# Attention branch sums finished in 32-row blocks on VectorE instead of by token through TensorE transposes

## Chip, core and metric

The kernel runs on one core of a Trainium2 chip. The metric is the device time of one execution in microseconds (us). A difference of less than about 0.3% cannot be told from none. The engines are TensorE (PE: matmuls and transposes, result in PSUM), VectorE (DVE), ScalarE (ACT), GpSimd (POOL, works on SBUF only here) and SyncE (SP, issues the DMAs).

## What is computed

The input x has 8 rows of 512 tokens of 256 numbers; everything is f32. It is normalised, and attention and a feed-forward part are added to it. Attention has 16 heads of 16 numbers and three branches: over 32 compressed keys (each made from 16 tokens), over the 4 best groups of 16 tokens, and over a causal window of 32 tokens back. Three gates per token weigh the branches.

```python
s_b = einsum('bhtd,bhnd->bhtn', q, k_c) / scale
logits_c = where(c_ok, s_b, NEG)                  # a group counts once it lies wholly in the past
out_c = einsum('bhtn,bhnd->bhtd', softmax(logits_c), v_c) * any(c_ok)
_, top_idx = top_k(logits_c, 4)                   # 4 groups of 16 tokens per query and head
out_s = ...                                       # softmax attention over the chosen tokens
wmask = (abs(pos[:, None] - pos[None, :]) <= 32) & (pos[:, None] >= pos[None, :])
out_l = einsum('bhts,bhsd->bhtd', softmax(where(wmask, q @ k / scale, NEG)), v)
gates = softmax(q.mean(axis=1) @ Wg + bg)         # three per token
out = gates[..., 0:1] * out_c + gates[..., 1:2] * out_s + gates[..., 2:3] * out_l
x = x + out @ Wo + ffn(xn)
```

The feed-forward part is a gated MLP of width 1024 and a product-key mixture over 1024 small experts (4 heads, 8 chosen of 64 x 64 pairs). The change does not touch it.

## The kernel before, in words

The work is cut into 8 rows and 32 blocks of 128 tokens (`tiles`: number `n`, position `i` = 0 to 3 in the row); the MLP goes by halves of a row. Each step is a Python generator (a stage), and `each` makes one chain per stage over its rows, blocks or halves. A planner, the `Conductor` (class before `tile_kernel`), holds a model of every engine's time: at each `yield` a stage says which engine and which buffers or events it needs next, `price` gives each instruction a length, and `run` issues the step that can begin first, the lower rank first among near ties. `PLAN` holds one number per item of each stage that shifts its rank. So prices and ranks fix, before the run, the order of the instructions in each engine's queue; on the chip each queue is worked strictly in that order. PSUM is handed out as two pairs of banks and four single banks (`pairs`, `banks`), SBUF buffers by `stock(name, count, shape)`.

The steps that matter here, for one block:

- `queries`: q, then the compressed logits: two matmuls of all 32 keys of 8 heads each, and a mask product; ACT copies them to `lg`.
- `select`: the maximum per head, the differences `ec` on POOL, the choice of the four groups.
- `compressed`: ACT takes exp of `ec`, PE turns it in four transposes (`ecT`), and four matmuls with `ecT` as the stationary operand multiply by `vc17`. The result lies by token (128 tokens in partitions, 17 numbers per head, the seventeenth the sum of the weights). DVE inverts the sums and scales by them and the gate: `atc`.
- `weights`: for the window (unit `None`) and for each key block: 16 matmuls of 32 rows by 128 columns (four heads side by side), exp on ACT into `wT`. To the window unit a band mask is added by four full 128x128 matmuls of an identity with `bandT`.
- `products`: `wT` times `v17` into two accumulator banks `acc[0]`, `acc[1]`. These have heads and numbers in partitions (32 per head group `g`: 16 numbers, then the sum of weights) and tokens in columns, for the two branches.
- `finish(0)` and `finish(1)`, through `by_token`: ACT copies an accumulator to `acs`, PE turns it by four transposes, DVE inverts the sums (`rzn`) and scales each branch by its gate (`at`), POOL adds the two branches and `atc`, PE turns the sum back by one transpose, ACT copies it to `attnT`.
- `project`: the experts' product and two matmuls with `attnT` into one bank, then DVE adds to `yo` and SP writes it out.

Per row, `prepare_values` makes `v17`, the copies of the 32 last tokens `vl17`, and `vc17`; `gates` makes `gt` (tokens in partitions; 3 gates by 4 blocks); `release_row` frees them. The line that the profile shows for nearly everything is that of the planner's helper (L202), so instructions are told apart by the names of their tiles.

Of the kernel before, what the change touches and what calls it, by code (L numbers as in the profile page):

```python
# [12 lines left out]
ALU = mybir.AluOpType  # L13
# [3 lines left out]
P = 128  # L17
# [25 lines left out]
    ("ident", P), ("any", 1), ("slot", 8), ("fold", 2 * P), ("head4", H), ("last", 2),  # L43
]
_BF_COLS = [
    ("identb", P), ("win", P + WIN), ("caus", P), ("causT", P), ("bandT", P), ("prevT", WIN),
# [17 lines left out]
def shape_constants():  # L64
# [21 lines left out]
    put("head4", p // NB == np.arange(H)[None] % 4)  # L86
# [6 lines left out]
    putb("bandT", np.where((q - p >= 0) & (q - p <= WIN), 0.0, OUT))  # L93
# [14 lines left out]
def bc(ap, axis, n):  # L108
# [8 lines left out]
    "-10",  # L117
    "-12",
    "-5 -5 2 -1 -3 -11 0 -1",
    "-30 5 0 -14 0 -5 12 -4",  # L120
    "0 7 6 -4 0 0 10 4",
    "-7 5 4 0 9 25 -10 6",
    "-1 3 -1 23 3 14 4 -30 -30 -2 -7 -11 -2 -20 4 3 -9 -6 30 1 3 -1 3 4 2 14 -7 2 6 -8 10 23",
    "-3 0 2 -4 8 0 0 -4 -2 0 -4 -1 -7 -4 1 0 3 2 0 -7 0 2 0 1 -21 -2 0 -3 23 -9 7 -10",
    "-1 0 24 30 12 4 10 0 29 4 -1 -30 5 3 1 0 20 26 6 30 0 9 1 13 18 -1 13 16 -10 16 28 21",
    "4 0 -5 0 0 3 3 -27 0 -5 -6 -30 -15 -28 2 -16 8 6 -13 9 -29 -25 0 -13 -17 12 3 -6 0 -14 28 "
    "2",
    "-1 7 7 0 11 -14 18 -30 0 -12 1 -12 -2 19 0 -7 8 0 0 0 7 0 6 -24 -24 -28 13 -19 10 -23 -21 "
    "7",
    "-19 -18 12 -8 0 -17 -3 -20 -19 3 1 0 -4 -14 -1 -12 -1 -26 9 2 7 5 -1 -2 3 -14 -9 -12 0 0 "  # L130
    "8 -11",
    "0 -4 -25 -23 4 -7 -17 -30 -30 -2 -1 -29 -13 -30 -2 -11 -24 0 -4 -27 -28 -30 9 -3 -9 -2 "
    "-27 0 0 -9 2 16",
    "0 -7 -21 -2 -1 -5 -7 -6 0 -30 0 -25 -3 -3 10 -3 7 0 17 15 6 12 0 0 0 2 22 5 29 -28 30 0",
    "-6 0 0 16 5 10 -8 5 17 -14 1 8 -26 -9 0 0 4 0 2 4 -10 -7 1 -3 14 -27 26 -3 15 2 -10 13",
    "-3 1 0 0 3 0 -3 -4 1 2 2 -30 0 -10 3 1 3 -5 0 -4 10 2 0 7 11 0 6 0 0 -2 14 28",
    "-14 9 -8 -1 -10 -3 1 27 -13 0 3 1 -7 1 -4 6 -12 -24 -2 1 3 -18 -6 7 21 1 -2 9 -13 0 4 15",
    "-2 -29 0 -7 3 -1 -30 0 0 -18 -3 0 11 0 11 -10 -12 0 -7 30 -27 -24 0 -3 -13 -1 16 8 1 -10 "
    "24 23",
    "-1 0 -10 0 0 -30 -7 18 -3 2 11 1 -11 11 -20 7 -7 4 0 7 8 -3 12 -5 0 4 -25 8 -25 0 -14 12",  # L140
    "20 1 0 -3 7 6 18 7 -18 4 -8 1 -14 -6 1 -8",
    "0 7 0 -7 0 -3 7 1 0 4 0 0 -2 -3 8 15",
    "-16 19 19 6 -10 6 -8 15 1 0 -5 1 7 6 12 21 -20 15 26 3 -4 -7 -1 -8 -9 -5 6 9 -9 -15 -25 0",
    "-28 10 -28 13 -3 0 4 -11 0 12 19 -21 -5 -14 28 -26 -2 0 26 17 13 -29 25 -23 17 0 0 26 -2 "
    "7 12 0",
# [60 lines left out]
class Conductor:  # L206
# [26 lines left out]
    def price(self, eng, op, args, kw):  # L233
# [3 lines left out]
        if eng == "PE":  # L237
            self.tiling = (P, P)
            if op == "transpose":
                cost = 0.109  # L240
            else:
                n = int(np.prod(args[2].shape[1:]))
                cost = n * 0.433e-3 if args[2].dtype == BF16 else max(n * 1.69e-3, 0.223)
                if self.share > 1:
                    k, m = args[1].shape[0], int(np.prod(args[1].shape[1:]))
                    self.tiling = tuple(32 if a <= 32 else 64 if a <= 64 else P for a in (k, m))
                    each = 1.05 if m > 32 else 0.97 if n > 64 else 1.25
                    cost = max(n * 0.423e-3 * each, 0.017)
        elif eng == "SP":
            cost = 0.36  # L250
        else:
# [4 lines left out]
            if eng == "POOL" and any(a.dtype == BF16 for a in aps):  # L256
                cost += 0.24e-3 * n
            if op in ("match_replace", "max_index", "tensor_tensor_reduce", "reciprocal"):
                cost += 0.08
# [69 lines left out]
def tile_kernel(ctx, tc, x, wq, wk, wqT, wv, wo, bdk, bdv, wga, bga, wgu, bg, bu, wd, bd,  # L329
# [64 lines left out]
    ident, identb = const("ident"), bconst("identb")  # L394
    cmask = bconst("cmask").rearrange("p (i n) -> p i n", n=NB)
# [37 lines left out]
    vc17s = stock("vc17_", 2, [P, H * D1])  # L433
    for st_, fill in ((v17s, 1.0), (vl17s, 0.0), (vc17s, 0.0)):
        for it in st_.items:
            pool.memset(it[0], fill)
# [5 lines left out]
    for it in vc17s.items:  # L442
        pool.tensor_copy(by_head(it[0])[:, :, D], const("head4"))
# [23 lines left out]
    gts = stock("gt", 3, [P, 3, NT])  # L467
# [8 lines left out]
    ecTs, acss = stock("ecT", 1, [P, 4, P]), stock("acs", 2, [P, 4, P])  # L476
    rzs = stock("rzn", 3, [P, 16])
    atcs, at2s = stock("atc", 2, [P, 16, D]), stock("at2", 2, [P, 2, 2, 4 * D])
# [178 lines left out]
    def gates(s, pg):  # L657

        s.gt = yield DVE, gts
        gt, gm = s.gt.ap, buf_gm  # L660
# [13 lines left out]
        vec.tensor_tensor(gt[:, 2, 0:1], gt[:, 2, 0:1], const("any"), ALU.mult)  # L674
        s.done("gates")
# [3 lines left out]
    def prepare_values(s):  # L679
# [53 lines left out]
        s.vc17 = yield None, vc17s  # L733
        vc17 = s.vc17.ap
        pt = yield PE, banks
        pvt = pt.ap[:, :2 * P].rearrange("p (c n) -> p c n", c=2)
        for f in range(2):
# [4 lines left out]
        vec.tensor_tensor(by_head(vc17)[:, :, :D], pvt.rearrange("p c (h d) -> p (c h) d", d=D),  # L742
                          bc(const("head4"), 2, D), ALU.mult)
# [7 lines left out]
    def release_row(s):  # L751
# [8 lines left out]
        for it in (s.vc17, s.v17, s.vl17):  # L760
            it.free()
        yield None, s.tiles[-1].ev("at0"), s.tiles[-1].ev("at1")
        s.gt.free()
# [3 lines left out]
    def queries(t):  # L767

        s, i = t.row, t.i
        yield None, s.ev("xn"), came["wq_s"]  # L770
# [13 lines left out]
        pt, t.lg = yield PE, banks, lgs  # L784
        for a in range(2):
            mm(pt.ap[:, a * 8 * NB:(a + 1) * 8 * NB], t.q.ap[:, a, :],
               s.kcbd.ap[:, a].rearrange("p h n -> p (h n)"), start=a == 0, stop=False,
               skip_group_check=True)
        pc = pt.ap.rearrange("p (h n) -> p h n", n=NB)
        first = i * (P // G)  # L790
        mm(pc[:, :, first:], identb, bc(cmask[:, i, first:], 1, H), start=False, stop=True,
           skip_group_check=True)
        yield ACT,
        act.copy(t.lg.ap[:, :, 4:], pc)
# [60 lines left out]
    def select(t):  # L855
# [13 lines left out]
        pool.tensor_tensor(t.ec.ap, lg[:, :, 4:], bc(mx, 2, NB), ALU.subtract)  # L869
# [68 lines left out]
    def by_token(acs, dst, gates):  # L938

        pt = yield PE, banks  # L940
        p4 = pt.ap.rearrange("p (a g d) -> p a g d", a=4, g=4)
        for a in range(4):
            pe.transpose(p4[:, a].rearrange("p g d -> p (g d)"), acs.ap[:, a, :], ident)
        acs.free()
        rzn = yield DVE, rzs
        po = p4.rearrange("p a g d -> p (a g) d")
        vec.reciprocal(rzn.ap, po[:, :, D])
        for b in range(2):
            c = slice(8 * b, 8 * b + 8)
            vec.scalar_tensor_tensor(dst[:, c], po[:, c, :D], gates[:, b:b + 1],  # L950
                                     bc(rzn.ap[:, c], 2, D), ALU.mult, ALU.mult)
        pt.free()
        rzn.free()

    def compressed(t):

        s, i = t.row, t.i
        yield ACT, t.ev("ec")
        act.activation(t.ec.ap, t.ec.ap, AF.Exp)
        pt, ecT = yield PE, banks, ecTs  # L960
        for g in range(4):
            pe.transpose(heads4(pt.ap)[:, g, :],
                         t.ec.ap[:, 4 * g:4 * g + 4, :].rearrange("p h n -> p (h n)"), ident)
# [4 lines left out]
        yield None, s.ev("vc"), s.ev("gates")  # L968

        pt = yield PE, banks  # L970
        w = 4 * D1
        for g in range(4):
            mm(pt.ap[:, g * w:g * w + w], ecT.ap[:, g, :], s.vc17.ap[:, g * w:g * w + w],
               start=g == 0, stop=g == 3, skip_group_check=True)
        ecT.free()
        t.done("pc")
        t.atc, t.attnT = yield None, atcs, attnTs
        rzn = yield DVE, rzs
        po = by_head(pt.ap[:, :H * D1])
        vec.reciprocal(rzn.ap, po[:, :, D])  # L980
        vec.scalar_tensor_tensor(t.atc.ap, po[:, :, :D], s.gt.ap[:, 2, i:i + 1], bc(rzn.ap, 2, D),
                                 ALU.mult, ALU.mult)
        pt.free()
        rzn.free()
        t.done("atc")

    def weights(t):
# [27 lines left out]
        for k in [None, *range(i // 2 * 2, i + 1), *range(i // 2 * 2)]:  # L1015
# [13 lines left out]
            mask = bconst("bandT") if k is None else bconst("causT")[:, :FEW] if i == 0 else None  # L1029
            if mask is not None:  # L1030
                for j in range(4):
                    mm(heads4(es[j // 2].ap[:, j % 2])[:, :, :mask.shape[-1]], identb, bc(mask, 1, 4),
                       start=False, stop=True, skip_group_check=True)
# [12 lines left out]
    def products(t):  # L1046
# [9 lines left out]
        accs = [a.ap.rearrange("p (b j q) -> p b j q", b=2, j=2) for a in acc]  # L1056
        for u in range(2 * (i + 2)):
# [3 lines left out]
            for jj in range(2):  # L1061
                for g in range(4):
                    c = D1 * (4 * g + 2 * jp + jj)
                    mm(accs[jp][32 * g:32 * g + 32, br, jj, :], v17[:n, kt, c:c + 32],
                       wT.ap[:n, jj, g, :], start=u < 2 and jj == 0, stop=False,
                       skip_group_check=True, tile_position=(0, 32 * g))
            wT.free()
            if u == 1 and i:
                for jp in range(2):
                    rows_ = slice(64 * jp, 64 * jp + 64)  # L1070
                    for jj in range(2):
                        for g in range(4):
                            c = D1 * (2 * g + jj)
                            mm(accs[jp][32 * g:32 * g + 32, 1, jj, :WIN], vl17[rows_, i - 1, c:c + 32],
# [6 lines left out]
    def finish(jp):  # L1081
        def body(t):
            s, i = t.row, t.i
            yield None, t.ev("pv"), t.ev("atc")
            acs, at2h = yield ACT, acss, at2s
            act.copy(acs.ap, heads4(t.acc[jp].ap))
            t.acc[jp].free()
            at2 = at2h.ap
# [329 lines left out]
```

## Time and profile before

| what | value |
|---|---|
| median of three timed executions | 1501.49 us (1499.8 to 1504.47) |
| the profiled execution's own time | 1506.37 us |
| its span, first to last instruction | 1504.3 us |
| mean granted TensorE clock | 0.989 |
| ACT, POOL busy | 649.0 us (43%), 962.5 us (64%) |
| DMA queue of the kernel's own transfers | 18.4% of 16 engines |

Busy time is the union of an engine's instructions, each from its start to its modelled end; consecutive instructions overlap by the pipeline's tail, so the mean length of one is more than what it costs in the queue. The chain that ended last is followed back from the last instruction, at each step to what released it. The group lines read: line, engine, operation, tile written <- tiles read, shape written <- shape read, count, then busy us, mean ns of one, then the idle time of the engine just before them and what ended most of it.

### The profile page before, as it was taken

How to read it: one execution, taken by the hardware profiler on the slowest of the kernel's cores; microseconds unless marked ns; L12 is line 12 of the kernel's file. 1: busy time of each engine (PE TensorE's matmuls, PEld its weight loads, DVE VectorE, ACT ScalarE, POOL GpSimd, SP SyncE). 2: the span in 40 equal slices, each digit the busy share in tenths (PEclk: the TensorE clock that was granted, in tenths of full speed). 3: DMA queues.
4: the chain of work that ended last, by engine and by line, in shares of the span. 5: the costliest groups of instructions: out<-in, count | busy, mean ns of one | idle time of the engine just before them, and what ended most of it. 6: DMA issues, size and time to landing. Idle time of an engine off the chain costs nothing.

```text
span 1504.3 us, 44379 instructions
## 1 busy us (share of the span) xinstructions
PE 1440.8 (96%) x17312; PEld 1126.9 (75%) x17312; DVE 1300.7 (86%) x5207; ACT 649.0 (43%) x1292; POOL 962.5 (64%) x948
## 2 busy tenths in 40 slices
PE   5899998999999999999999999999999999999999
PEld 4677777777777777777877778777877777877777
DVE  3989889979989988899889896989798978999992
ACT  3534451544354445452544425444434435344253
POOL 3546756755567566874675756777636775577676
PEclk9899999999999999999999999999999999999999
DMA  8111111212112112121122212022120112111120
GB/s 287 44 45 50 36 53 32 80 46 60 47 31 79 45 43 58 51 62 51 30 61 62 60 47 62 25 67 59 48 66 26 55 48 60 52 27 52 37 59 19
DMA packets 100018, 83.52 MB, mean 56 GB/s; under 512 B 23265, under 2 KB 80609, under 8 KB 99681
## 3 DMA queue, kind: packets, MB, share of 16 engines
q1 hardware_dynamic: 99808, 80.69, 18.4%
q8 instruction: 136, 2.23, 0.6%
q14 instruction: 74, 0.60, 0.1%
HBM read 49.67 MB, written 4.19 MB: 36 GB/s over the span
## 4 chain that ended last, share of the span: by engine, by line
PE 66%; DVE 24%; ACT 3%; issue 2%; POOL 2%; DMA 2%; SPq 0%; DVEq 0%; ACTq 0%; POOLq 0%
PE psum L202 66%; DVE bm L202 3%; DVE pick L202 2%; DVE big L202 1%; POOL big L202 1%; DVE sums L202 1%; DVE chosen L202 1%; DVE ml L202 1%; DVE at_x L202 1%; DVE aT L202 1%; ACT wT L202 1%; DVE hT L202 1%; DVE xg L202 1%; DVE mr L202 1%; DVE at L202 1%
## 5 line engine op out<-in xcount | busy, mean ns | idle before, releaser
L202 POOL TENSOR_TENSOR big<-chosen,ed 128x1024 f32<-128x1024 bf16 x128 | 275.1, 2149 | 250.1 <-DVE chosen L202 164.6
L202 ACT ACTIVATE wT<-psum 128x1024 f32<-128x1024 f32 (+1 forms) x224 | 218.4, 1024 | 149.6 <-PE psum L202 140.5
L202 PE MATMUL psum<-xnT,wb 128*128 128x256 f32 x1024 | 250.4, 388 | 9.2 <-DVE hT L202 6.9
L202 POOL TENSOR_TENSOR big<-big,ed 128x1024 f32<-128x1024 f32 x128 | 248.6, 1942 | 9.9
L202 PEld LDWEIGHTS psum<-xnT,wb 128*128 128x128 f32 x1024 | 187.4, 191 | 45.4 <-DVE hT L202 9.2
L202 DVE TENSOR_REDUCE bm<-psum 128x32 f32<-128x512 f32 (+2 forms) x224 | 199.5, 912 | 18.6 <-PE psum L202 18.2
L202 POOL TENSOR_TENSOR big<-big 128x512 f32<-128x512 f32 x128 | 141.0, 1102 | 9.6
L202 PE MATMUL psum<-wT,v 128*32 128x128 f32 (+1 forms) x3584 | 127.6, 278 | 7.4 <-ACT wT L202 5.3
L202 ACT ACTIVATE xg<-psum,bg_s 128x256 f32<-128x256 f32 x128 | 60.9, 476 | 162.0 <-PE psum L202 160.4
L202 PEld LDWEIGHTS psum<-xnT,deT_s 128*128 128x128 f32 x1024 | 122.1, 193 | 10.5 <-issue 4.9
L202 PE MATMUL psum<-xnT,deT_s 128*128 128x128 f32 x1024 | 127.0, 277 | 0.0
L202 PE MATMUL psum<-wd_s,hT 128*128 128x256 f32 x512 | 124.7, 387 | 1.2 <-DVE hT L202 0.8
L202 PE MATMUL psum<-ue_s,aT 128*128 128x256 f32 x512 | 121.8, 384 | 0.2 <-DVE aT L202 0.2
L202 PEld LDWEIGHTS psum<-wT,v 128*32 128x32 f32 (+1 forms) x3584 | 90.5, 110 | 40.3 <-ACT wT L202 16.5
L202 DVE SCALAR_TENSOR_TENSOR aT<-aT,psum 128x512 f32<-128x512 f32 x128 | 86.6, 680 | 27.3 <-ACT aT L202 23.5
L202 PEld LDWEIGHTS psum<-ue_s,aT 128*128 128x128 f32 x512 | 94.0, 190 | 21.3 <-issue 5.4
L202 PEld LDWEIGHTS psum<-wd_s,hT 128*128 128x128 f32 x512 | 94.0, 192 | 20.6 <-issue 4.2
L202 PE MATMUL psum<-k,q 32*128 32x384 f32 (+3 forms) x1024 | 98.0, 474 | 5.8 <-DMA k<-kT 5.7
L202 DVE TENSOR_TENSOR chosen<-rc 128x1024 bf16<-128x1024 bf16 x128 | 99.4, 776 | 0.0
L202 POOL TENSOR_TENSOR gw<-big 128x256 f32<-128x256 f32 x128 | 90.6, 707 | 10.0
L202 PE MATMUL psum<-qx,k 32*128 32x128 f32 (+1 forms) x2560 | 94.3, 282 | 1.8 <-ACT wT L202 1.3
L202 PEld LDWEIGHTS psum<-qx,k 32*128 32x128 f32 (+1 forms) x2560 | 78.4, 182 | 21.9 <-issue 14.6
(158 smaller groups left out, 2911.3 us busy)
## 6 DMA issues: line engine op xcount, KB each, us to landing
wb<-in_wgu SPq DMA_DIRECT2D x128, 256.0 KB, 2.7
qx<-qT SPq DMA_DIRECT2D x96, 64.0 KB, 1.9
qx<-xT SPq DMA_DIRECT2D x96, 64.0 KB, 1.9
yo<-in_x SPq DMA_DIRECT2D x32, 128.0 KB, 2.1
q<-qT SPq DMA_DIRECT2D x64, 64.0 KB, 2.0
k<-kT SPq DMA_DIRECT2D x16, 256.0 KB, 2.5
out<-yo SPq DMA_DIRECT2D x32, 128.0 KB, 1.7
kw<-k SPq DMA_DIRECT2D x48, 80.0 KB, 2.5
```

Source lines behind the costliest of these rows:

```text
L202: return f(*a, **k)
```

## The change

`by_token` and its ten transposes per block are gone. The accumulators' columns are laid out in four blocks of 32 tokens, so that a DVE transpose of 32x32 blocks puts 32 tokens into the 32 partitions of each head group. The compressed product is made in the same layout: `vcq` is now the stationary operand and `ecT` streams. Three such turns fill `accT` (branch, token block, head in the group, 32 numbers). A new stage `join` inverts all 48 sums in one reciprocal, multiplies by the gates, has POOL scale all three branches and add them, and turns the sum back with a fourth DVE transpose straight into `attnT`. The gates are needed per head group and token block, so `gates` has SP copy them in 16 small transfers per row into `gx`. The rows of Wo are put in the new order on the host.

The band mask becomes sixteen 32x32 matmuls, each on its own tile of the array. `queries`, `select` and `compressed` work on the `nb` = 8(i+1) compressed keys that block `i` can see, where they had all 32. The planner has two new prices, and `PLAN` is replaced in all 23 stages and has a 24th for `join`.

```diff
-    ("identb", P), ("win", P + WIN), ("caus", P), ("causT", P), ("bandT", P), ("prevT", WIN),
+    ("identb", P), ("win", P + WIN), ("caus", P), ("causT", P), ("bandR", 4 * P), ("prevT", WIN),
...
+                if self.share > 4:
+                    cost = max(n * 0.433e-3 / 16, 0.017)
...
+            if eng == "POOL" and op == "memset":
+                cost = 0.08 + 0.85e-3 * n
...
-    vc17s = stock("vc17_", 2, [P, H * D1])
+    vcqs = stock("vcq", 2, [P, 4, P])
...
-    gts = stock("gt", 3, [P, 3, NT])
+    gts, gxs = stock("gt", 1, [P, NT, 3]), stock("gx", 3, [P, 4, NT, 3])
...
-    ecTs, acss = stock("ecT", 1, [P, 4, P]), stock("acs", 2, [P, 4, P])
-    rzs = stock("rzn", 3, [P, 16])
-    atcs, at2s = stock("atc", 2, [P, 16, D]), stock("at2", 2, [P, 2, 2, 4 * D])
+    ecTs, accTs = stock("ecT", 1, [P, 4, P]), stock("accT", 1, [P, 3, 4, 4, 32])
+    rz3 = buf("rz3", [P, 3, 4, 4])
+    ats = stock("at", 1, [P, 16, D])
...
+        s.gx = yield SP, gxs
+        for c in range(4):
+            for g in range(4):
+                sp.dma_start(out=s.gx.ap[32 * g:32 * g + 32, c], in_=gth.ap[32 * c:32 * c + 32])
...
         for a in range(2):
-            mm(pt.ap[:, a * 8 * NB:(a + 1) * 8 * NB], t.q.ap[:, a, :],
-               s.kcbd.ap[:, a].rearrange("p h n -> p (h n)"), start=a == 0, stop=False,
-               skip_group_check=True)
-        pc = pt.ap.rearrange("p (h n) -> p h n", n=NB)
+            mm(pc[:, 8 * a:8 * a + 8], t.q.ap[:, a, :], s.kcbd.ap[:, a, :, :nb], start=a == 0,
+               stop=False, skip_group_check=True)
         first = i * (P // G)
-        mm(pc[:, :, first:], identb, bc(cmask[:, i, first:], 1, H), start=False, stop=True,
+        mm(pc[:, :, first:], identb, bc(cmask[:, i, first:nb], 1, H), start=False, stop=True,
            skip_group_check=True)
...
-    def by_token(acs, dst, gates):
-
-        pt = yield PE, banks
-        p4 = pt.ap.rearrange("p (a g d) -> p a g d", a=4, g=4)
-        for a in range(4):
-            pe.transpose(p4[:, a].rearrange("p g d -> p (g d)"), acs.ap[:, a, :], ident)
...
-        w = 4 * D1
-        for g in range(4):
-            mm(pt.ap[:, g * w:g * w + w], ecT.ap[:, g, :], s.vc17.ap[:, g * w:g * w + w],
-               start=g == 0, stop=g == 3, skip_group_check=True)
+        pc = pt.ap.rearrange("p (b j q) -> p b j q", b=4, j=4)
+        for j in range(4):
+            mm(pc[:, :, j, :], s.vcq.ap[:, j, :], ecT.ap[:, j, :].rearrange("p (b q) -> p b q", b=4),
+               start=j == 0, stop=j == 3, skip_group_check=True)
         ecT.free()
         t.done("pc")
...
+        t.accT = yield DVE, accTs
+        vec.transpose(t.accT.ap[:, 2].rearrange("p b j m -> p (b j m)"), pt.ap)
         pt.free()
...
-            mask = bconst("bandT") if k is None else bconst("causT")[:, :FEW] if i == 0 else None
-            if mask is not None:
+            if k is None:
+                con.share = 16
+                for c in range(4):
+                    for j in range(4):
+                        r = slice(32 * j, 32 * j + 32)
+                        mm(heads4(es[j // 2].ap[32 * c:32 * c + 32, j % 2]), identb[r, r],
+                           bc(bandR[r, c], 1, 4), start=False, stop=True, skip_group_check=True,
+                           tile_position=(32 * j, 32 * c))
+                con.share = 1
...
-            yield None, t.ev("pv"), t.ev("atc")
-            acs, at2h = yield ACT, acss, at2s
-            act.copy(acs.ap, heads4(t.acc[jp].ap))
+            yield DVE, t.ev("pv"), t.ev("acc2")
+            vec.transpose(t.accT.ap[:, 0:2, :, 2 * jp:2 * jp + 2, :].rearrange("p r b j m -> p r b (j m)"),
+                          t.acc[jp].ap.rearrange("p (r b n) -> p r b n", r=2, b=4))
             t.acc[jp].free()
...
+    def join(t):
+
+        s, i = t.row, t.i
+        yield None, s.ev("gates")
+        yield DVE, t.ev("acc0"), t.ev("acc1")
+        acc = t.accT.ap.rearrange("p r b j m -> p r (b j) m")
+        vec.reciprocal(rz3.rearrange("p r b j -> p r (b j)"), acc[:, :, :, D])
+        vec.tensor_tensor(rz3, rz3, bc(s.gx.ap[:, :, i, :].rearrange("p b r -> p r b"), 3, 4), ALU.mult)
+        t.done("rz")
+        yield POOL,
+        part = t.accT.ap.rearrange("p r b j m -> p (r b j) m")[:, :, :D]
+        pool.tensor_tensor(part, part, bc(rz3.rearrange("p r b j -> p (r b j)"), 2, D), ALU.mult)
+        pool.tensor_tensor(acc[:, 0, :, :D], acc[:, 0, :, :D], acc[:, 1, :, :D], ALU.add)
+        ath = yield POOL, ats
+        at = ath.ap
+        pool.tensor_tensor(at, acc[:, 0, :, :D], acc[:, 2, :, :D], ALU.add)
+        t.accT.free()
+        t.attnT = yield DVE, attnTs
+        vec.transpose(t.attnT.ap.rearrange("p a (b q) -> p b a q", b=4),
+                      at.rearrange("p (b a j) d -> p b a (j d)", b=4, a=2))
+        ath.free()
+        t.done("attn")
...
-        yield PE, t.ev("attn0"), t.ev("attn1")
+        yield PE, t.ev("attn")
...
+    each(tiles, lambda t: t.n + 0.24, join)
```

## Prediction

> **What bounds the kernel now.** I read the page's busy table first, then the chain that ended last, then the timeline of one block's end, then the groups with shapes kept apart.
>
> ```profile
> PE 1440.8 (96%) x17312; PEld 1126.9 (75%) x17312; DVE 1300.7 (86%) x5207; ACT 649.0 (43%) x1292; POOL 962.5 (64%) x948
> ...
> PE 66%; DVE 24%; ACT 3%; issue 2%; POOL 2%; DMA 2%; SPq 0%; DVEq 0%; ACTq 0%; POOLq 0%
> ```
>
> TensorE (PE) has work for 96% of the span and owns 66% of the chain. VectorE (DVE) is second in both: 86% and 24%. So work taken from PE should show, and work given to DVE is dear. The table by stretches says how dear:
>
> ```profile
> 400.00:600.00 200.00, 193.99 (x2544) 151.10 (x2542) 180.61 (x732) 92.33 (x179) 126.80 (x123) 1.00 0.18 50
> 600.00:800.00 200.00, 196.98 (x2323) 153.33 (x2322) 178.59 (x749) 88.34 (x178) 133.56 (x133) 1.00 0.17 49
> ```
>
> (columns: length, then busy us of PE, its weight loads, DVE, ACT, POOL, then clock, DMA share, GB/s). In the body PE is at 97 to 98% and DVE at 89 to 90%. The clock is 1.00, so there is nothing to win from it. Over 40 to 1400 us the rows sum to PE 1317.6 and DVE 1211.1 of 1360: 97% and 89%.
>
> **The removed end of a block**, in the timeline (start, length, engine, what):
>
> ```profile
> 673.53 1.07 ACT L202 COPY acs<-psum 128x512 f32<-128x512 f32 x2
> 674.94 0.91 PEld L202 LDWEIGHTS psum<-cst,acs 128*128 128x128 f32 x8
> 675.05 1.04 PE L202 MATMUL psum<-cst,acs 128*128 128x128 f32 x8
> 675.69 0.26 DVE L202 RECIPROCAL rzn<-psum 128x16 f32<-128x16 f32 x1
> 675.98 0.61 DVE L202 SCALAR_TENSOR_TENSOR at<-psum,gt,rzn 128x128 f32<-128x128 f32 x2
> 676.67 0.45 POOL L202 TENSOR_TENSOR at<-at 128x128 f32<-128x128 f32 x1 [1.16 <-DVE at L202]
> ```
>
> A "mean ns of one" on PE (276 for this form) holds a pipeline tail that the next matmul overlaps; what one costs in the queue is the spacing: 1.04 us for eight, of which the last one's length is 0.273, so 0.767/7 = 0.110 us each.
>
> **PE, per block of 128 tokens (32 blocks).**
> - Ten transposes go (two times four of acs, two of at): 10 x 0.110 = 1.10 us.
> - The band mask is four 128x512 bf16 matmuls now: four in 1.04 us in the timeline, (1.04 - 0.39)/3 = 0.217 each, 0.87 in all. It becomes sixteen matmuls of 32 rows x 32 columns that stream 512 columns each. The trace has 32x32 tiles only with 32 columns: 32 of them in 0.45 us, or 11.3 us for 768, 15 ns each. Lower bound: issue, 16 x 0.015 = 0.24. Upper bound: the four column groups take turns, 4 x 0.217 = 0.87, no gain. I take issue of most of them plus one stream, about 0.40, nearer to the row of its own tile shape; gain 0.47, bounds 0 to 0.63.
> - Against this stands the Trainium skill, "TensorE: Matmul & The Clock Gate", section "Why this matters for your kernels": sixteen 32x32 tiles at 512 columns measured 660 ns as a set. By it the gain is 0.21 instead of 0.47, and the whole sum 8 us smaller; no row here shows the set.
> - Compressed logits: four passes of 256 columns per block at 0.217 (the kcbd group) become 64, 128, 192 or 256 columns by block position. A 128-column pass has a spacing of 0.11 (the deT_s group, 127.0 us for 1024, tails included) and I allow no less for 64. Gain 4 x (0.107 + 0.107 + 0.054 + 0)/4 = 0.27. Their mask falls from 512/384/256/128 to 128 columns: mean gain 0.08.
> - The vc product streams 128 columns instead of 68. Both sit at the 0.11 floor: 0. The products keep their columns, only in blocks of 32: 0.
> - Sum 1.10 + 0.47 + 0.27 + 0.08 = 1.92 us; x 32 = **61 us off PE** (bounds 46 to 66).
>
> **DVE.** These three groups go:
>
> ```profile
> L202 DVE SCALAR_TENSOR_TENSOR at<-psum,gt,rzn 128x128 f32<-128x128 f32 x128 | 39.0, 347 | 2.6
> L202 DVE RECIPROCAL rzn<-psum 128x16 f32<-128x16 f32 x96 | 24.0, 250 | 17.0 <-PE psum L202 16.6
> L202 DVE SCALAR_TENSOR_TENSOR atc<-psum,gt,rzn 128x256 f32<-128x256 f32 x32 | 15.5, 484 | 1.4
> ```
>
> 78.5 us. In their place, per block: three 32x32-block turns of 128x512 out of PSUM, one of 128x256 out of SBUF, one reciprocal and one product of 128x48. The trace has no turn. The rows that read the same 128x512 from PSUM are 680 (aT) and 683 ns (bm), the 128x256 SBUF reduction is 418. If the turn passes an element as these do, 3 x 0.68 + 0.42 = 2.46. From below I see no reason for less than the 593 ns in which ACT copies such a bank, 0.27 less per block, 9 us in all. From above the DVE row with the most time per element is the contended pick product, 873 ns for 256, 3.4 ns per element: 1792 elements x 2.4 ns more = 4.3 us per block. I take 2.46, nearest in source and shape. The Trainium skill, "Vector Engine (DVE) Microarchitecture Reference", section 3.8 on the reshape front end, says the turn sustains one element per cycle per lane; by its rate the middle value holds, and no run here shows it. The reciprocal lies between 0.25 (16 elements) and 0.46 (rising on as from 4 elements at 173 to 16 at 250): 0.33. The product lies between 265 (32 elements) and 374 (64): 0.32. Sum 3.11 x 32 = 99.5; net **+21 us on DVE**, 1322 in all (bounds +8 to +165).
>
> **ACT, POOL, SP.** ACT loses acs (35.5) and attnT (17.0) and parts of the ec and lg passes: about 58 us off an engine at 43%; worth nothing by itself, but wT exponentials start sooner behind it. POOL loses its two at groups (33.9 + 32.3) and about 10 us of ec (1104 ns at 512 elements, 707 at 256). It gains per block a product of 768 elements (between 1102 at 512 and 1942 at 1024: 1.52) and two adds of 256 (0.707 each): 2.93 x 32 = 94. Net +18 us on an engine with 540 us idle: nothing, if DVE doesn't wait for it. The cover is project's slack; without it each block would pay these 2.9 us plus route's 2.1 us operation ahead in POOL's queue.
>
> SP gets sixteen small transfers a row for the spread gates, 128 in all, at about 0.35 us of queue each (the nearest issues, out<-yo, take that in the timeline): 5.6 us per row, landing about 2 us later (rows: 1.7 to 2.7). They stand in SP's queue behind a wait for the gates (PE, ACT, DVE), and what is queued behind them is qx, q, kw and wb. The SP queue's own waits are mostly for PE (463.5 us) and for yo (230.7), so it has room. In the timeline the last row's gates are done at 1311 us and the next acs copy starts at 1340: 29 us, against 8 needed. Uncovered, it is up to 8 us per row, 64 in all.
>
> The new waits: finish waits on DVE for the products and the compressed turn, and join on POOL's result before the last turn; with one accT and one at buffer, the next block's compressed turn is queued behind the join before it. Blocks are 1504/32 = 47 us apart and the whole end (2 x 0.68 + 0.33 + 0.32 + 2.93 + 0.42 and six hand-overs at about 0.15) is 6.3 us. Accumulator banks come free after a 0.68 DVE turn instead of a 0.59 ACT copy, in a busier queue: late here means PE waits for a bank. Against it, four bank uses per block (two by-token, two at) are gone. At the tail of the run the new end is about 1 us longer than acs at 1492.0 to the at transposes at 1496.5.
>
> **The sum.** The profiled execution took 1506.4 (span 1504.3 and 2.1 around it). If PE's gain counted only where PE is on the chain and DVE's addition where DVE is: -0.66 x 61 + 0.24 x 21 = -35, so 1471. If all of it counted, and PE's direct waits for the removed groups too (at, acs and attnT, about 8 us): -69, so 1437. The order is searched anew for these lengths, and the two engines are now nearer to each other, which pull opposite ways; I take the middle, -52: 1454. The runs shown have a median of 1501.5, 4.9 below the profiled one; so **1449**, -3.5%.
>
> **Rivals.**
> 1. *DVE becomes the bound.* In the stretch of 1360 us, PE's gain alone would leave about 1304 us, and DVE's 1211 + 19 = 1230 would be 94% of it, where it has 89% now and sits in 24% of the chain. If it cannot be kept above 92%, the stretch is 1337, the gain 23: 1479. For it: PE's longest waits in the body are for DVE and ACT results. Against it: slices with 9 in the DVE row are already half of the page's 40.
> 2. *The turn is slow, so the kernel is.* Place: DVE, 1792 turned elements per block. Each extra ns per element costs 57 us. It decides from the point where DVE reaches PE's 96% of the old span, 1440 us: 118 us more than my 1322, 2.1 ns more, some 3.1 ns per element. At 3.5 ns DVE has 1465 us, and at 96% the span is 1526, about 1523 timed. For it: no row shows a turn, and the upper bound above lies past that point. Against it: every plain DVE row from PSUM is near 1.3 ns per element with its fixed part.
> 3. *All of it counts, and the order also closes PE's stalls.* PE's 63 us of idle time shrink by some 15: 1437 - 15 - 5 = 1417.
> 4. *The sixteen mask tiles take turns* (the change doesn't do what it says): 15 us of the gain gone, 1449 + 13 = 1462, inside the forecast's own range (1430 to 1467).
>
> **Chances.** Forecast with rival 4: 0.62. DVE bound (1467 to 1497): 0.18. Better than forecast: 0.08. Nothing to be told apart (within 0.3%, 4.5 us, about what a measurement here can tell): 0.02. Slower: 0.10. The range 1423 to 1490 leaves out the slower cases, no change, and the ends of the others, about 0.2. Faster 0.88, same 0.02, slower 0.10.
>
> **What would show it.** A turn's mean near 680 ns; the mask set's sixteen within about 0.4 us; PE busy near 1380 with a share still at 95% or more, DVE near 1320 and 91%; the PE share of the chain falling and DVE's rising. If DVE's share passes 94% and PE's falls under 93%, rival 1 holds. I am wrong if turns take over a microsecond, if SP's queue waits for gates show up as DVE waits for gx, or if PE waits for banks that DVE still holds.

## The result: 1587.7 us, slower by 5.7%, and the profile after

The changed kernel takes 1587.68 us (median; 1586.91 to 1591.32) beside 1502.98 for the kernel before on the same chip: ratio 1.0565 (1.0529 to 1.06). 1449 was forecast. The profiled execution has a span of 1586.7 us, and a mean granted clock of 0.966, down from 0.989. The busy table after:

```profile
PE 1435.9 (91%) x17376; PEld 1109.2 (70%) x17376; DVE 1358.1 (86%) x5143; ACT 593.3 (37%) x1164; POOL 985.9 (62%) x924
```

No engine has gained share. PE's idle time (span less busy) went from 63.5 to 150.8 us, +87.3, while its busy time fell by 4.9: these two are the 82.4 us by which the span grew. DVE has 57 us more work, but the same 86%, so it hasn't become a full engine either. Where this happens is read from PE's 40 slices, each 39.7 us, and from the clock below them:

```profile
PE   5999999999999899999989878997987989877997
...
PEclk8999999999999999999999979999999999998899
```

Behind the start, the first 20 slices hold one 8; in the 20 after them, that is from 793 us on, 12 are at 7 or 8. The table by stretches, with the prediction's columns, says it in numbers:

```profile
400.00:600.00 200.00, 191.11 (x2217) 153.06 (x2216) 191.73 (x688) 77.70 (x159) 134.53 (x123) 0.98 0.18 52
600.00:800.00 200.00, 190.75 (x2577) 149.73 (x2577) 169.66 (x638) 86.25 (x163) 124.20 (x115) 1.00 0.20 57
800.00:1000.00 200.00, 172.70 (x2052) 130.27 (x2051) 164.14 (x602) 66.92 (x130) 117.16 (x110) 0.91 0.13 38
1000.00:1200.00 200.00, 181.07 (x1960) 141.75 (x1958) 180.66 (x708) 72.48 (x155) 123.18 (x115) 0.97 0.19 54
1200.00:1400.00 200.00, 175.51 (x2108) 132.59 (x2109) 161.47 (x622) 69.15 (x137) 123.09 (x112) 0.98 0.14 41
```

The kernel before, in its own stretches from 800 us on, has no such loss:

```profile
800.00:1000.00 200.00, 196.19 (x2398) 155.73 (x2397) 173.41 (x661) 88.76 (x175) 136.98 (x133) 1.00 0.19 53
1000.00:1200.00 200.00, 195.93 (x2310) 153.75 (x2309) 177.07 (x725) 89.28 (x179) 122.38 (x122) 0.99 0.18 52
1200.00:1400.00 200.00, 193.75 (x2420) 152.00 (x2417) 183.23 (x739) 85.39 (x169) 134.90 (x129) 1.00 0.18 50
```

From 400 to 800 us PE is at 95% after the change; in the three stretches behind that it is at 86, 91 and 88%, and DVE, at 96 and 85% up to 800 us, is at 82, 90 and 81%. Each row of four blocks has the same operations, in the first half of the run as in the second. So the new operations as such don't explain the loss: something that differs between the halves does. In two of the three late stretches no engine is near full, which an unfit order of the queues could do. In the list of waits no single new hand-over stands out:

```profile
ACT wT L204 <- PE psum L204: 187.5, 105, 8.4
POOL big L204 <- DVE chosen L204: 187.2, 68, 13.1
...
POOL accT L204 <- DVE rz L204: 79.4, 14, 20.2
...
DVE accT L204 <- PE psum L204: 45.0, 15, 9.7
```

(engine and tile, what it waited for, us in total, times, longest). The old waits have grown, ACT for PE from 140.5 to 187.5 and POOL for `chosen` from 164.6 to 187.2; POOL's wait for the join's `rz` and DVE's wait for a product to turn are new; the first stands where POOL waited 73.1 us for DVE's `at` before.

### The profile page after: what moved, and what is told of

Read it like the earlier page. It is cut to its first block, busy times and chain, and to the rows that moved or that the text cites. A ratio compares the mean times of both kernels' runs of the same rounds, so it can differ in the third digit from the quotient of the medians.

```text
span 1586.7 us, 44446 instructions
## 1 busy us (share of the span) xinstructions
PE 1435.9 (91%) x17376; PEld 1109.2 (70%) x17376; DVE 1358.1 (86%) x5143; ACT 593.3 (37%) x1164; POOL 985.9 (62%) x924
## 5 line engine op out<-in xcount | busy, mean ns | idle before, releaser
L204 POOL TENSOR_TENSOR big<-chosen,ed 128x1024 f32<-128x1024 bf16 x128 | 276.6, 2161 | 277.0 <-DVE chosen L204 187.2
L204 ACT ACTIVATE wT<-psum 128x1024 f32<-128x1024 f32 (+1 forms) x224 | 218.3, 1023 | 187.7 <-PE psum L204 187.5
L204 DVE TENSOR_REDUCE bm<-psum 128x32 f32<-128x512 f32 (+2 forms) x224 | 198.5, 909 | 14.2 <-PE psum L204 13.7
L204 PE MATMUL psum<-wT,v 128*32 128x128 f32 (+1 forms) x3584 | 131.1, 280 | 18.7 <-ACT wT L204 16.0
L204 PE MATMUL psum<-xnT,deT_s 128*128 128x128 f32 x1024 | 131.6, 283 | 5.6 <-DVE aT L204 4.5
L204 PEld LDWEIGHTS psum<-xnT,deT_s 128*128 128x128 f32 x1024 | 125.4, 198 | 15.6 <-DVE aT L204 5.6
L204 PE MATMUL psum<-k,q 32*128 32x384 f32 (+3 forms) x1024 | 116.7, 480 | 13.6 <-DVE ml L204 7.6
L204 PE MATMUL psum<-ue_s,aT 128*128 128x256 f32 x512 | 126.1, 389 | 1.3 <-DVE aT L204 0.8
L204 DVE SCALAR_TENSOR_TENSOR aT<-aT,psum 128x512 f32<-128x512 f32 x128 | 86.4, 678 | 26.1 <-PE psum L204 17.2
L204 PEld LDWEIGHTS psum<-ue_s,aT 128*128 128x128 f32 x512 | 94.2, 192 | 19.9 <-issue 4.5
L204 DVE STREAM_TRANSPOSE accT<-psum 128x512 f32<-128x512 f32 x96 | 65.2, 697 | 46.6 <-PE psum L204 45.0
L204 PE MATMUL psum<-qx,k 32*128 32x128 f32 (+1 forms) x2560 | 98.8, 287 | 1.5 <-DMA qx<-xT 1.3
L204 POOL TENSOR_TENSOR accT<-accT,rz 128x768 f32<-128x768 f32 x32 | 48.6, 1518 | 80.4 <-DVE rz L204 79.4
```

The lines of the kernel that those rows point to most:

```text
L204: return f(*a, **k)
```

## What the experiments test

**Theory "order".** The planner sorts by rank, and `PLAN` shifts an item's rank by whole tenths: `rank(it) + 0.1 * d`. Route's block 14 has 14.2 + 0.1 x 29 = 17.1, and so have compressed's block 14, logits 15, experts 16, hidden 9 and residual 17; extend 17 has 17.099999999999998 in floating point. Compressed's block 23 has 26.2 (26.200000000000003), and so has experts 23. How such a tie falls depends on the last bit or, where that is equal too, on the place in a list. `PLAN` gives many more equal ranks; only these two are turned below. All that is planned behind a tie follows from it, so numbers of `PLAN` that suit one outcome needn't suit the other. The planner's own model gives a hint, a modelled length and not a measured time: it ends at 1436.1 for before, at 1485.0 for after, and at 1378.9 for after with both of these ranks lowered by a millionth.

**Rivals.** "DVE": its added 57 us bind. "Hand-over": the join's path through DVE, POOL and DVE stalls the end of each block. "Parts": what is saved on PE isn't worth its length, in whatever order.

## Experiments on the order

**e_ties** is the changed kernel with the two ranks lowered; no instruction is added or taken away.

```diff
-                con.cur.rank = rank(it) + 0.1 * d
+                con.cur.rank = rank(it) + 0.1 * d - 1e-6 * (
+                    (body, it.__dict__.get('n')) in ((route, 14), (compressed, 23)))
```

> The changed kernel with two ranks lowered by a millionth, so that two ties in the planner (route of block 14, compressed of block 23) fall the other way; nothing else differs, and every instruction is the same. Theory O (the loss is the order): the shift list was made for the other outcome of these ties and everything planned after the first one is mistuned; the kernel's own planner ends at 1378.9 instead of 1485.0, and since before stands 66 us over its planner's end of 1436.1, the time is about 1445 (1430 to 1465), faster than before. Theory D (VectorE is the bound): the order matters little, 1560 or more. Theory J (the join with one buffer holds up the next block): as D, 1550 or more.

1497.47 us, ratio 0.9964 (0.9947 to 0.9981): 90 us less than after. That refutes D and J, which had 1550 or more; the same join in another order does not cost the 90 us. But theory O's own range, 1430 to 1465, is missed by 32 us: the order explains the slowdown and not the whole distance to the forecast. PE's idle time is 92.4 instead of 150.8. Its stretches from 800 us on, where after had 172.70, 181.07 and 175.51:

```profile
800.00:1000.00 200.00, 191.53 (x2420) 148.71 (x2419) 189.02 (x727) 82.08 (x163) 141.79 (x131) 0.98 0.18 52
1000.00:1200.00 200.00, 184.78 (x2155) 143.26 (x2152) 187.17 (x702) 75.25 (x150) 134.64 (x124) 0.97 0.17 47
1200.00:1400.00 200.00, 191.66 (x2402) 148.42 (x2401) 183.44 (x682) 72.65 (x143) 145.51 (x129) 0.99 0.15 45
```

Its stretch of 400 to 600 us has PE at 191.12, after at 191.11: the two run alike until the tie. DVE's timeline, first of e_ties, then of after, shows the point where they part:

```profile
705.86 0.39 DVE L204 TENSOR_TENSOR yo<-psum,yo 128x256 f32<-128x256 f32 x1
706.17 0.67 DVE L204 TENSOR_TENSOR chosen<-rc 128x1024 bf16<-128x1024 bf16 x1
706.76 1.21 DVE L204 TENSOR_REDUCE bm<-psum 128x64 f32<-128x1024 f32 x1
```

```profile
705.79 0.38 DVE L204 TENSOR_TENSOR yo<-psum,yo 128x256 f32<-128x256 f32 x1
706.10 1.21 DVE L204 TENSOR_REDUCE bm<-psum 128x64 f32<-128x1024 f32 x1
...
709.58 0.69 DVE L204 TENSOR_TENSOR chosen<-rc 128x1024 bf16<-128x1024 bf16 x1
```

Route's `chosen` (block 14, the first tie) goes ahead of the maxima (`bm`, of logits 15) in the one, 3.4 us later in the other. That alone is small; but from there on every later decision of the planner is another one.

**e_tie14** turns only the first tie.

```diff
+                con.cur.rank = rank(it) + 0.1 * d - 1e-6 * (
+                    (body, it.__dict__.get('n')) == (route, 14))
```

> Only the first of the two ties (route of block 14) is turned. Theory O: the planner ends at 1439.9; the body runs as in the run with both ties up to block 23 and loses from there on, about 1505 to 1530. Theories D and J: no different from the changed kernel, about 1588.

1551.83 us, 1.0316 (1.0277 to 1.0355). Theory O's 1505 to 1530 is missed, D's and J's 1588 as well. The first tie is worth 36 us, the second another 54. The model has this order at 1439.9, 3.8 above before; on the chip it is 49 us above. So the model's end isn't a forecast.

**a_plan0** and **b_plan0** are the changed kernel and the kernel before with every string of `PLAN` empty, so both are ordered by the same plain ranks.

```diff
-    (stage): "(its numbers)"
+    (stage): ""
```

> The changed kernel with the list of shifts emptied in all stages: the order is what the base ranks give. Theory O: worse than the changed kernel, since its first half is still tuned; 1600 to 1640, and 20 to 50 us faster than the kernel before with an emptied list. Theory D: about as slow as the changed kernel (1570 to 1600), and slower than the kernel before with an emptied list, because the body itself is slower.

> The kernel before with the list of shifts emptied. Theory O: its tuned list is worth over 100 us, 1630 to 1680. Theory D: order is worth little, under 1560.

1614.3 (1.0743, 1.0706 to 1.0779) and 1643.12 us (1.093, 1.0892 to 1.0968), both as theory O had them. Two readings. The order that before has is worth 140 us to it; the one that after has is worth only 27 to it, though the same body with two ranks turned gains 117. And with plain ranks the new body is 28.8 us shorter than the old one (0.9825; 0.976 to 0.990 by the ends of the two intervals). That is one order each, and orders differ by tens of us, so it is a hint that the operations are no loss, not a price.

## Experiments on the size of the gain

With the two ties turned, the gain is 5.4 us, little more than the 0.3% that can be told, where 52 were forecast. The next runs look for the rest. Where an instruction is replaced, the planner still books the old one, so the order is held.

**b_parts** is before with the sixteen-tile mask and the short compressed logits and exponentials: 0.47 + 0.27 + 0.08 us per block by the prediction, 26 us in all, without the join. Its edit, condensed (brackets stand for code that is left out):

```diff
-   (four 128x128 mask matmuls, logits over 32 keys)
+   con.book("PE", "matmul", (the old operands), {})
+   nc.tensor.matmul(heads4(es[j // 2].ap[32*c:32*c+32, j % 2]), identb[r, r], bc(bandR[r, c], 1, 4),
+                    start=False, stop=True, skip_group_check=True, tile_position=(32*j, 32*c))
```

> The kernel before, with only the two parts of the change that take work from TensorE and give VectorE none: the mask as sixteen tiles, and the compressed logits and exponentials cut to the visible keys. The new instructions are issued where the planner placed the old ones, so the order is that of before. Theory O with TensorE as the bound of before: my 26 us for these parts (0.82 us in 32 blocks) come off nearly whole, 1476 to 1485. Theory D (VectorE sets the time already): under 10 us, 1493 to 1503.

1495.32 us, 0.9952 (0.9935 to 0.9969). PE's busy time and the chain after it:

```profile
PE 1420.5 (95%) x17696; PEld 1114.6 (75%) x17696; DVE 1297.2 (87%) x5207; ACT 637.2 (43%) x1292; POOL 956.9 (64%) x956
...
PE 59%; DVE 32%; issue 3%; ACT 3%; POOL 1%; DMA 1%; SPq 0%; DVEq 0%; ACTq 0%; POOLq 0%
```

The work is gone (-20.3 us busy), the time isn't (-7.2): the chain went over from PE (66 to 59%) to DVE (24 to 32%). By its expectation this speaks for D, VectorE as the bound.

**b_pe2** is before with the four mask matmuls issued twice, 28 us by their spacing.

```diff
+                for add in (mm, nc.tensor.matmul) if k is None else (mm,):
+                    add(...the mask...)
```

> The kernel before with the four band-mask matmuls of each block issued twice, the order held: 28 us more on TensorE. Theory B and P: 20 us or more, 1522 to 1540. Theory V: under 10 us.

1522.96 us, 1.0129 (1.011 to 1.0148): PE busy +24.5, time +20. This speaks against V, VectorE alone as the bound.

**b_dveless** and **e_dveless** are before and e_ties with the window's maximum taken over every fourth of its 160 columns, so three quarters of that reduction are left out. **b_both** is b_parts with the same.

```diff
-    vec.tensor_tensor_reduce(out=junk, in0=..., in1=...)
+    con.book("DVE", "tensor_tensor_reduce", (), dict(out=junk, in0=..., in1=...))
+    nc.vector.tensor_tensor_reduce(out=junk[:, ::4], in0=sp_[:, jj, 0, lo::4], in1=bconst("win")[:, ::4], ...)
```

> The kernel before with work taken from VectorE alone, the order held: the window's maximum (256 operations, only the softmax's reference value) is taken over every fourth of its 160 columns, which leaves out three quarters of that reduction; by 120 columns at 0.96 GHz-like spacing (0.244 us for 160 columns now) some 25 to 32 us of VectorE go. Theory V (VectorE alone sets the time of before): most of it comes off, 1470 to 1482. Theory B (TensorE and VectorE hold each other up by turns, so that what one gains waits for the other): 5 to 15 us, 1487 to 1498. Theory P (TensorE alone): under 4 us.

> The changed kernel with both ties turned and the same shortened window maximum (it leaves out the same three quarters of that reduction), the order held. With TensorE lighter by 61 us, VectorE is the later of the two: 15 to 30 us off 1497.5, a larger part of the work removed than in the kernel before (theory B), 1468 to 1483. If the order's mismatch alone keeps it slow: under 8 us.

> The run with TensorE's two parts (7 us gained for 26 us of work) and the shortened window maximum together, the order held. Theory B: more than the sum of the two alone, 25 to 40 us off, 1463 to 1478. Theory V: no more than the shortened maximum alone.

1499.13 us (0.998, 0.9968 to 0.9992), 1488.85 (0.9914, 0.9895 to 0.9932) and 1489.19 (0.991, 0.9893 to 0.9926). 20 us less DVE work save 3 in before (0.2%, under the 0.3% that can be told from none), which is theory P's outcome; 22 us save 8.6 in e_ties, where DVE has the larger share, and 15 to 30 had been expected. So cutting either engine's work alone gains little, and no theory of one bound fits all of b_parts, b_pe2 and b_dveless. Taken together PE's and DVE's cuts save 13.3, a bit more than 7.2 + 3, but theory B had 25 to 40, and 21.8 us of PE and 28.1 of DVE are gone from the busy times: two engines that hold each other up are part of the matter, but not enough of it.

**e_dve2** is e_ties with each of the 96 turns out of PSUM issued twice; **b_dve2** is before with each of its 128 scalings `at` issued three times.

```diff
+    nc.vector.transpose(...)                                      # e_dve2: once more
...
-            vec.scalar_tensor_tensor(dst[:, c], ...)
+            for scale in (vec, nc.vector, nc.vector):             # b_dve2
+                scale.scalar_tensor_tensor(dst[:, c], ...)
```

> The changed kernel with both ties turned, with each of the 96 turns out of PSUM issued twice (the second writes the same again), the order held: 59 us more on VectorE. If VectorE binds beside TensorE now (38% of the chain): 25 to 50 us more, 1520 to 1550. If TensorE still binds: under 15 us more.

> The kernel before with the 128 scalings by token issued three times each, the order held: 67 us more on VectorE. If TensorE sets the time of before (VectorE 24% of the chain): 10 to 25 us more, 1513 to 1528, a third of the added work or less. If VectorE binds as hard there as in the changed kernel: 35 us or more, as large a part of the added work as in the run that doubles the turns.

1546.05 us (1.0282, 1.0252 to 1.0312) and 1602.56 (1.0669, 1.0639 to 1.07). In e_dve2, 58.1 us more of DVE work cost 48.6, and the chain turns over; the first line is that of e_ties, the second that of e_dve2:

```profile
PE 50%; DVE 38%; POOL 3%; issue 3%; ACT 2%; DMA 2%; SPq 2%; DVEq 0%; POOLq 0%; ACTq 0%
...
DVE 50%; PE 39%; issue 4%; POOL 3%; ACT 2%; SPq 1%; DMA 1%; DVEq 0%; POOLq 0%; ACTq 0%
```

For b_dve2 the 10 to 25 us were missed by far, and the other branch (35 or more, as large a part as in e_dve2) was passed too: 85.5 us cost 100. The by-token end of before is a path in which PE's transposes stand behind DVE, POOL and ACT, so a longer DVE step there is paid for in PE's queue too. In its waits POOL's for `at`, 73.1 us before, and PE's for `at`, 3.2 us before, have become (L951 is the line of the two scalings that are added):

```profile
POOL at L202 <- DVE at L951: 136.1, 49, 9.3
...
PE psum L202 <- DVE at L951: 35.7, 34, 3.0
```

## Experiments on GpSimd beside VectorE

**e_poolrz** is e_ties with the join's product of 128x48 on POOL, right ahead of the product that needs it.

```diff
-        vec.tensor_tensor(rz3, rz3, bc(s.gx...), ALU.mult)
+        con.book("DVE", "tensor_tensor", (rz3, rz3, gx3, ALU.mult), {})
+        nc.gpsimd.tensor_tensor(rz3, rz3, gx3, ALU.mult)
```

> The changed kernel with both ties turned, and join's product of the sums with the gates (0.62 us each on VectorE, 20 us in all) issued on GpSimd instead, at the same place in the order. If VectorE's work and its waits behind GpSimd have taken the place that TensorE had, part of the 20 us comes off: 1485 to 1492 against 1497.5. If the order alone is to blame, or TensorE still sets the time: no change within 4 us.

1490.22 us, 0.9912 (0.9887 to 0.9938), as expected, and the shortest of the kernels that leave nothing out. Moving products of 17.2 us off DVE gains about 7 over e_ties, while DVE's busy time falls by 9.3 and POOL's rises by 8.6. What stretched the product shows in the tile's own view in e_ties (count, then minimum, median and maximum of one in ns, first and last start):

```profile
L204 DVE TENSOR_TENSOR rz<-rz,gx x32: 207/209/1950, 86.1 to 1486.5; 128x48 f32<-128x48 f32 x32
L204 POOL TENSOR_TENSOR accT<-accT,rz x32: 1485/1494/2403, 86.4 to 1486.8; 128x768 f32<-128x768 f32 x32
```

The median product takes 209 ns, the longest 1950: about the length of one of POOL's large operations (1940 ns for 128x1024). The timeline of e_ties shows what such a one waits for:

```profile
277.35 2.14 POOL L204 TENSOR_TENSOR big<-chosen,ed 128x1024 f32<-128x1024 bf16 x1 [2.59 <-DVE chosen L204]
...
277.61 1.95 DVE L204 TENSOR_TENSOR rz<-rz,gx 128x48 f32<-128x48 f32 x1
```

POOL's operation ends at 279.49 us, DVE's product at 279.56. So it is with all 13 of the 32 that took more than 240 ns: each began while an operation of POOL ran, and ended 56 to 67 ns after that one. They make the mean of 536.

**b_pool2** is before with one more POOL product of 768 elements per block, on scratch that nothing reads. **e_lesspool** is e_ties without the join's product of 768 and its first addition (the branches aren't scaled, and one isn't added).

```diff
+        if jp == 1:                                               # b_pool2
+            nc.gpsimd.tensor_tensor(scr, scr, bc(scr1, 1, 48), ALU.mult)
...
-        pool.tensor_tensor(part, part, ..., ALU.mult)             # e_lesspool, both only booked
-        pool.tensor_tensor(acc[:, 0, :, :D], acc[:, 0, :, :D], acc[:, 1, :, :D], ALU.add)
+        con.book("POOL", ...)
```

> The kernel before with one GpSimd product of 768 elements more per block, on scratch, behind the second at sum, the order held: 48 us more on GpSimd. Theory W: VectorE's busy time rises by 8 us or more with the same instructions and the time by 8 to 25 us, 1510 to 1527. If GpSimd has room at 64%: under 4 us.

> The changed kernel with both ties turned, the order held, and join's product of 768 elements and its first addition on GpSimd left out (the branches are not scaled, only one addition is done): 2.3 us per block, 73 us less on GpSimd, nothing less on VectorE. Theory W (VectorE's operations with both operands in SBUF stand waiting while GpSimd works, and the new GpSimd work made them longer): VectorE's busy time falls by 15 us or more without an instruction less, and the time by 10 to 25 us, 1472 to 1488. If GpSimd is off the path: under 4 us, VectorE's busy time the same.

1526.4 us (1.0147, 1.0122 to 1.0171) and 1490.1 (0.99, 0.9872 to 0.9928). In b_pool2 nobody waits for the scratch, and DVE has the same instructions as in before, but its busy time, 1300.7 there, is:

```profile
PE 1444.5 (95%) x17312; PEld 1127.9 (74%) x17312; DVE 1322.6 (87%) x5207; ACT 649.0 (43%) x1292; POOL 1024.0 (67%) x982
```

61 us of POOL work on an engine with 540 us to spare lengthened DVE's busy time by 21.9 us, and the whole by 22. But the second doesn't follow from the first alone. What stands in POOL's queue behind the scratch product starts later, and that is waited for. The chain, with POOL at 2% in before, and PE's wait for POOL's `at`, 0.7 us in before, are now:

```profile
PE 53%; DVE 27%; POOL 11%; issue 3%; ACT 3%; DMA 2%; SPq 1%; POOLq 0%; DVEq 0%; ACTq 0%
...
PE psum L202 <- POOL at L202: 12.2, 11, 2.4
```

How the 22 us divide between the two isn't shown. In e_lesspool POOL is 78.3 us shorter, DVE 12.8 with the same instructions, the time 7.4 (15 or more and 10 to 25 had been expected); the join is shorter there too, so this run doesn't divide them either.

## Why the prediction was wrong

**The step that failed** is in the sum: "The order is searched anew for these lengths, and the two engines are now nearer to each other, which pull opposite ways; I take the middle, -52". It took for granted that the new order is as fit for the new lengths as the old one was for the old. e_ties shows that two ranks lowered by a millionth are worth 90 us, with not one instruction changed. No rival had this: the one that ended slower than before was a slow turn, and turns were not slow. None of the prediction's signs of being wrong came up either: turns took 0.70 us, DVE waited 1.5 us for `gx` in after, and PE waited 15.0 us in after and 3.0 in e_ties for banks that a turn still held. That the numbers of `PLAN` were made with these ties falling the other way is what the model's 1378.9 against 1485.0 suggests; it is inferred, not shown.

**The second failure is the size of the gain**: with the ties turned -5.4 us is left of -52. The sum had the gain between -35, with each engine's change at its share of the chain, and -69. The runs show another rule for an order that is held: added work costs 0.8 to 1.2 of its length (b_pe2 20 of 24.5, e_dve2 48.6 of 58.1, b_dve2 100 of 85.5), removed work returns 0.15 to 0.4 (b_parts 7.2 of 20.3, b_dveless 3 of 19.9, e_dveless 8.6 of 22.3). "If PE's gain counted only where PE is on the chain" was thus no lower bound. A chain share prices neither: DVE's additions cost 0.84 of their length at 38% of the chain (e_dve2) and 1.17 at 24% (b_dve2), and a removal uncovers the next chain at once (b_parts). The sum counted 0.66 to 1 of PE's removal and at most 0.24 of DVE's addition. With 0.36 and 0.84 it would be -0.36 x 61 + 0.84 x 21 = -4, near the -5.4 of e_ties; but these rates are from held orders, so that fits and proves nothing. A free order may return more than a held one, as the 28.8 of the pair with plain ranks hint.

Point by point:

- *PE, 61 us off.* The parts that the trace can show came true. The mask set, in the timeline of e_ties:

```profile
441.12 1.17 PE L204 MATMUL psum<-qx,kw 32*128 32x128 f32 x32
442.22 0.43 PE L204 MATMUL psum<-cbf 32*32 32x512 bf16 x16
442.58 0.44 PE L204 MATMUL psum<-cst,xn 128*128 128x128 f32 x2
```

  Sixteen tiles take 0.43 us from start to end, and the next matmul starts 0.36 us after the first of them; 0.40 was taken, and rival 4 (0.87) falls. The 660 ns that the Trainium skill gives for the set ("TensorE: Matmul & The Clock Gate", "Why this matters for your kernels") is not what it costs in this queue. Short logits have means of 281, 283, 337 and 391 ns for 64 to 256 columns in after, so 64 are no cheaper than 128, as allowed for. Busy time fell by 38.4 us in e_ties and by 4.9 in after; in both it contains matmuls stretched by a lower clock (0.978 and 0.966, 0.989 before), so it is no clean measure of the 61.
- *DVE, +21.* The turn was right: 697 ns for 128x512 from PSUM and 435 for 128x256 (0.68 and 0.42 taken); rival 2 falls. The reciprocal took 445 ns, near the upper bound of 0.46 and not at 0.33; the product 621 in after and 536 in e_ties against 0.32, by way of POOL. These two are 10.5 us over in e_ties. Most of what is left of its +42.8 is in instructions that the change doesn't touch: some became shorter, but `sums<-top` went from 828 to 1070 ns and `at_x<-at_x,cnt` from 741 to 983, 7.8 us each. In after the sum is +57.
- *POOL, "nothing, if DVE doesn't wait for it".* The condition failed, though not as a wait that the profile lists: DVE's operations with both inputs in SBUF last longer beside POOL's, the join's product until POOL's is done. In b_pool2 added POOL work cost 0.36 of its length, by DVE's longer operations and by POOL's own queue together. The Trainium skill states the mechanism ("SBUF — State Buffer", "Who interferes with whom"): a VectorE instruction with two SBUF inputs contends with a GpSimd instruction that reads SBUF. The runs agree, and the turns speak for it as well: reading PSUM, none of the 96 in e_ties took more than 717 ns (at least 666), where the product that reads SBUF twice took from 207 to 1950.
- *ACT, -58*: 55.7 in after. *SP and the gates*: DVE waited 1.5 us for `gx` in all; the cover held. *Clock, "nothing to win from it"*: true, but there was something to lose. Span times one less clock, an estimate of what the lower clock costs, is 16.5 us before, 32.9 in e_ties, 53.9 in after.
- *Rival 1, DVE as the bound,* gave 1479, nearer to the 1497 of e_ties than the forecast was, and DVE's part of the chain rose to 38%. But by its own sign (DVE over 94%, PE under 93%) it does not hold: DVE is at 90% and PE at 94%.

**What stays open.** The 48 us between forecast and e_ties aren't split item by item among the DVE operations beside POOL, the clock, and the order. The model that made the order expects -57 from before to e_ties (1378.9 - 1436.1), like the forecast, and the chip gives -5. Its prices hold no clock. DVE's waiting for POOL they do hold (`book` puts off a DVE operation on SBUF that would begin while POOL works), so that term isn't missing from the model; whether it is too small there wasn't measured. Whether an order made with corrected prices would return more wasn't tried.

## What to carry to other kernels

Where a planner fixes the order before the run, an edit of the body is an edit of the order, and the order can be worth more than the edit: here 90 us hung on two ties that no instruction count shows. Keep a plan's keys free of ties, and compare two bodies under an order that both are equally fit or unfit for. With queues worked in order and two engines above 85%, removed work was worth 0.4 of its length or less here, and added work nearly all of it or more: count them so, and not by the shares of the chain.

## What the runs showed of the hardware

- Work on GpSimd whose result nobody reads isn't free: 61 us of it raised VectorE's busy time by 22, with the same instructions; 78 us taken away lowered it by 13. A 128x48 product of 209 ns took up to 1950: each of the 13 long ones in e_ties ended 56 to 67 ns after the GpSimd operation beside which it began.
- Sixteen 32x32 matmul tiles of 512 columns take 0.36 us of TensorE's queue, where four 128x128 ones took 0.87.
- The granted clock was mostly lower where PE was busy for a smaller share: 0.989 at 96% (before), 0.978 at 94% (e_ties), 0.966 at 91% (after), 0.954 at 90% (a_plan0), and 0.91 in the stretch of 800 to 1000 us of after, with PE at 86%. The share alone doesn't set it: b_parts and e_lesspool both have PE at 95%, at 0.990 and 0.972.
